# The attention rows issue in the order of the source

## The chip, the cores and the metric

The kernel runs on one core of one Trainium2 chip. The metric is the device time in microseconds of one execution. The kernel before takes 3320.47 us (median of three runs, 3319.91 to 3330.44).

## The reference, cut to what matters

Two layers follow one another on an image `x` of 256 x 256 pixels with 128 channels. Each adds its result to its input. Layer 0 is attention along each row of the image, with a bias and a gate; layer 1 is a spectral network, which the change does not touch.

```python
def _L0_conv_ref(q_x, kv_x, bias1, bias2, wq, wk, wv, wg, bg, wo, bo):
    H = 4; C_HIDDEN = 32
    q = split_heads(einsum('...qi,oi->...qo', q_x, wq)) / np.sqrt(C_HIDDEN)
    k = split_heads(einsum('...ki,oi->...ko', kv_x, wk))
    v = split_heads(einsum('...ki,oi->...ko', kv_x, wv))
    a = einsum('bshqd,bshkd->bshqk', q, k)
    a = a + bias1 + bias2
    a = softmax(a, axis=-1)
    o = einsum('bshqk,bshkd->bshqd', a, v)
    g = sigmoid(einsum('...qi,oi->...qo', q_x, wg) + bg)
    o = o * g                      # o and g laid out by head
    return einsum('...qi,oi->...qo', o, wo) + bo

x = x + _L0_conv_ref(_gn(x), kv_x, bias1, bias2, wq, wk, wv, wg, bg, wo, bo)
x = x + _L1_conv_ref(_gn(x), ...)      # layer 1, spectral
```

`s` is the row of the image: 256 independent rows, each with 256 queries, 256 keys and 4 heads.

## The kernel before, in the parts that matter

All is in 32-bit floats. Before the rows, a first stage reads the image for the group statistics (`mr`) and prepares the transposed bias as `exp(bias)` in `b1T`. Then 256 rows are worked in a software pipeline: pass `i` of the loop computes the scores of row `i`, projects row `i + 1`, transposes row `i + 2`, weighs row `i`, does the output projection of row `i - 3`, the first transform of layer 1 for row `i - 4`, and the sum over values of row `i - 1`.

```python
ps_s = tile_pool(name="l0s", bufs=1, space=PSUM)   # scores: two tiles of 128 x 1024
ps_a = tile_pool(name="l0a", bufs=4, space=PSUM)   # all else: one tag "a", four buffers

def turn(s):                                       # tr
    ps = ps_a.tile([P, 512], FP, tag="a", name=f"tr_{s}")
    for j in range(2):
        nc.tensor.transpose(ps[:, j * P : (j + 1) * P], r["x"][:, j, :], ident)
        nc.tensor.transpose(ps[:, 256 + j * P : 256 + (j + 1) * P], r["kv"][:, j, :], ident)
    nc.scalar.activation(r["xnT"], ps[:, 0:256], AF.Identity, bias=self.nmr, scale=self.mr[:, 1:2])
    nc.scalar.copy(r["kvT"], ps[:, 256:512])

def project(s):
    ps = ps_a.tile([P, 512], FP, tag="a", name=f"qk_{s}")
    nc.tensor.matmul(ps[:, 0:256], wT["wq"], xnT, start=True, stop=True)
    nc.tensor.matmul(ps[:, 256:512], wT["wk"], kvT, start=True, stop=True)
    nc.scalar.copy(r["qkT"], ps)
    ps = ps_a.tile([P, 512], FP, tag="a", name=f"gv_{s}")
    for c in range(2):
        nc.tensor.matmul(ps[:, 256 + c * P : 256 + (c + 1) * P], kvT[:, c * P : (c + 1) * P], wT["wv"], ...)
    nc.tensor.matmul(ps[:, 0:256], wT["wg"], xnT, start=True, stop=True)
    nc.vector.tensor_copy(r["v"], ps[:, 256:512])
    nc.scalar.activation(r["gate"], ps[:, 0:256], AF.Tanh, bias=self.hbg, scale=0.5)
    if s > 0:
        rows[s - 1].pop("exp")(1, 1)               # the fourth exponential of the row before

def scores(s):
    # 8 matmuls into sc[0] (heads 0, 1) and sc[1] (heads 2, 3), each by halves c of the keys
    ...
    exp(0, 0); exp(0, 1); exp(1, 0)                # on ACT; exp(1, 1) comes in project(s + 1)
    nc.vector.tensor_tensor(r["e"][0], sc[0], b1T[:, 0:2], ALU.mult)

def weigh(s):
    nc.gpsimd.tensor_tensor(e1, e1, b1T[:, 2:4], ALU.mult)
    for hp in (1, 0):
        nc.gpsimd.tensor_tensor(r["es"][hp], e[:, :, 0, :], e[:, :, 1, :], ALU.add)

def attend(s):
    ps = ps_a.tile([P, 512], FP, tag="a", name=f"av_{s}")
    # 8 matmuls of v with e into ps[:, 0:256], 4 of ones with es into ps[:, 256:512]
    ...
    nc.vector.scalar_tensor_tensor(t, r["gate"], 1.0, ps[:, 0:256], ALU.add, ALU.mult)
    nc.vector.reciprocal(rd, rd)                   # rd = ps[:, 256:512]
    nc.vector.scalar_tensor_tensor(t, rd, SUM_SCALE, t, ALU.mult, ALU.mult)
    nc.gpsimd.tensor_tensor(r["x1"], r["x"], bc(self.bo, 1, 2), ALU.add)

def out(s):                                        # ps is "wo": 2 matmuls of og with wo
    nc.vector.tensor_tensor(r["x1"], ps[:, 0:256], r["x1"], ALU.add)
    nc.sync.dma_start(self.x1d[s], r["x1"])

def spectrum(s):                                   # ps is "u": 2 transposes, 2 matmuls with adft
    nc.vector.bn_stats(self.stats2[:, s, :], ps[:, 0:256])
    nc.scalar.copy(self.U[:, :, s], ps[:, 256 : 256 + 129])
```

(Shapes are shortened, and cuts are marked with dots.) The order in which an engine gets its instructions is not the order of this text: a scheduler, working ahead of time from an estimate of each instruction's length, chooses the order on every engine and inserts the waits that data and buffers need. In each pass ScalarE (ACT in the profile) has four exponentials, the copies `qkT`, `xnT`, `kvT` and U, and the gate.

Of the kernel before, what the change touches and what calls it, by code (L numbers as in the profile page):

```python
# [11 lines left out]
AF = mybir.ActivationFunctionType  # L12
ALU = mybir.AluOpType
AX = mybir.AxisListType
PSUM = bass.MemoryType.PSUM
DRAM = bass.MemoryType.DRAM

# [141 lines left out]
class Rows:  # L159
# [4 lines left out]
    SG = 2  # L164
# [55 lines left out]
    def run(self):  # L220
        tc, NS, SG = self.tc, self.NS, self.SG
        nc = tc.nc
        ctx, wT, ident, rows = self.ctx, self.wT, self.ident, self.rows
# [5 lines left out]
        def turn(s):  # L229
            r = rows[s]  # L230
# [4 lines that stand above are left out]
            r["xnT"] = wk.tile([P, 256], FP, tag="xnT", name=f"xnT_{s}")  # L235
            nc.scalar.activation(r["xnT"], ps[:, 0:256], AF.Identity, bias=self.nmr, scale=self.mr[:, 1:2])  # L236
            r["kvT"] = wk.tile([P, 256], FP, tag="kvT", name=f"kvT_{s}")
            nc.scalar.copy(r["kvT"], ps[:, 256:512])

        def project(s):  # L240
            r = rows[s]
            xnT, kvT = r["xnT"], r["kvT"]
# [3 lines that stand above are left out]
            r["qkT"] = wk.tile([P, 512], FP, tag="qkT", name=f"qkT_{s}")  # L246
# [3 lines that stand above are left out]
                nc.tensor.matmul(  # L250
                    ps[:, 256 + c * P : 256 + (c + 1) * P], kvT[:, c * P : (c + 1) * P], wT["wv"],
                    start=True, stop=True,
                )
            nc.tensor.matmul(ps[:, 0:256], wT["wg"], xnT, start=True, stop=True)
            r["v"] = wk.tile([P, 2, P], FP, tag="v", name=f"v_{s}", bufs=3)
            nc.vector.tensor_copy(r["v"].rearrange("p c d -> p (c d)"), ps[:, 256:512])
            r["gate"] = wk.tile([P, 256], FP, tag="gate", name=f"gate_{s}", bufs=3)
            nc.scalar.activation(r["gate"], ps[:, 0:256], AF.Tanh, bias=self.hbg, scale=0.5)  # L258
            if s > 0:
                rows[s - 1].pop("exp")(1, 1)  # L260

        def scores(s):

            r = rows[s]
            qkT = r["qkT"]
            sc = [ps_s.tile([P, 2, 512], FP, tag=f"s{hp}", name=f"sc_{s}_{hp}") for hp in range(2)]
            for c in range(2):
                for h in range(4):
                    p = slice(32 * h, 32 * h + 32)
                    nc.tensor.matmul(  # L270
                        sc[h // 2][:, h % 2, c * 256 : (c + 1) * 256],
                        qkT[p, 256 + c * P : 256 + (c + 1) * P], qkT[p, 0:256],
                        start=True, stop=True,
                    )
            r["e"] = [wk.tile([P, 2, 2, 256], FP, tag=f"e{hp}", name=f"e_{s}_{hp}") for hp in range(2)]

            def exp(hp, c):
                z = sc[hp][:, :, c * 256 : (c + 1) * 256]
                nc.scalar.activation(  # L279
                    r["e"][1][:, :, c, :] if hp else z, z, AF.Exp, bias=b2T[:, c, s : s + 1]  # L280
                )

            exp(0, 0)
            exp(0, 1)
            exp(1, 0)
            r["exp"] = exp
            nc.vector.tensor_tensor(  # L287
                r["e"][0].rearrange("p h c q -> p (h c q)"), sc[0].rearrange("p h x -> p (h x)"),
                b1T[:, 0:2].rearrange("p h c q -> p (h c q)"), ALU.mult,
            )  # L290

        def weigh(s):

            r = rows[s]
            e1 = r["e"][1].rearrange("p h c q -> p (h c q)")
            nc.gpsimd.tensor_tensor(e1, e1, b1T[:, 2:4].rearrange("p h c q -> p (h c q)"), ALU.mult)  # L296
            r["es"] = [wk.tile([P, 2, 256], FP, tag=f"es{hp}", name=f"es_{s}_{hp}") for hp in range(2)]
            for hp in (1, 0):
                e = r["e"][hp]
                nc.gpsimd.tensor_tensor(r["es"][hp], e[:, :, 0, :], e[:, :, 1, :], ALU.add)  # L300

        def attend(s):
            r = rows[s]
            ps = ps_a.tile([P, 512], FP, tag="a", name=f"av_{s}")
            for c in range(2):
                for h in range(4):
                    hd = slice(32 * h, 32 * h + 32)
                    nc.tensor.matmul(  # L308
                        ps[hd, 0:256], r["v"][:, c, hd], r["e"][h // 2][:, h % 2, c, :],
                        start=(c == 0), stop=(c == 1),  # L310
                    )
            for h in range(4):
                nc.tensor.matmul(  # L313
                    ps[32 * h : 32 * h + 32, 256:512], self.ones, r["es"][h // 2][:, h % 2, :],
                    start=True, stop=True,
                )
            rd = ps[:, 256:512]
            t = r["og"] = wk.tile([P, 256], FP, tag="og", name=f"og_{s}", bufs=3)
            nc.vector.scalar_tensor_tensor(t, r["gate"], 1.0, ps[:, 0:256], ALU.add, ALU.mult)  # L319
            nc.vector.reciprocal(rd, rd)  # L320
            nc.vector.scalar_tensor_tensor(t, rd, SUM_SCALE, t, ALU.mult, ALU.mult)  # L321

            r["x1"] = wk.tile([P, 2, P], FP, tag="x1", name=f"x1_{s}", bufs=4)
            nc.gpsimd.tensor_tensor(r["x1"], r["x"], bc(self.bo, 1, 2), ALU.add)  # L324

        def out(s):
            r = rows[s]
            ps = ps_a.tile([P, 512], FP, tag="a", name=f"wo_{s}")
            for j in range(2):
                nc.tensor.matmul(  # L330
                    ps[:, j * P : (j + 1) * P], r["og"][:, j * P : (j + 1) * P], wT["wo"],
                    start=True, stop=True,
                )
            nc.vector.tensor_tensor(
                r["x1"], ps[:, 0:256].rearrange("p (j c) -> p j c", j=2), r["x1"], ALU.add
            )
            nc.sync.dma_start(self.x1d[s].rearrange("(p j) c -> p j c", j=2), r["x1"])

        def spectrum(s):
            x1 = rows[s]["x1"]  # L340
            ps = ps_a.tile([P, 512], FP, tag="a", name=f"u_{s}")
            for j in range(2):
                nc.tensor.transpose(ps[:, j * P : (j + 1) * P], x1[:, j, :], ident)
            for j in range(2):
                nc.tensor.matmul(  # L345
                    ps[:, 256 : 256 + 129], x1[:, j, :], self.adft[:, j, :], start=(j == 0), stop=(j == 1)
                )
            nc.vector.bn_stats(self.stats2[:, s, :], ps[:, 0:256])
            nc.scalar.copy(self.U[:, :, s], ps[:, 256 : 256 + 129])

        turn(0)
        turn(1)
        project(0)
        for i in range(NS + 4):
            if i % SG == 0 and i // SG + 2 < NS // SG:
                self.load(i // SG + 2)
            if i < NS:
                scores(i)
            if i + 1 < NS:
                project(i + 1)  # L360
            elif i < NS:
                rows[i].pop("exp")(1, 1)
            if i + 2 < NS:
                turn(i + 2)
            if i < NS:
                weigh(i)
            if 8 <= i < 16:
                k, h = divmod(i - 8, 4)
                nc.vector.tensor_reduce(
                    self.bad[:, k, h : h + 1], b1T[:, h].rearrange("p c q -> p (c q)"), AX.X,  # L370
                    ALU.min if k else ALU.max,
                )
            if 0 <= i - 3 < NS:
                out(i - 3)
            if 0 <= i - 4 < NS:
                spectrum(i - 4)
                del rows[i - 4]
            if 0 <= i - 1 < NS:
                attend(i - 1)


def layer0_general(tc, I, ident, x1d, U, stats2, wT, mr, bg, adft):
# [1180 lines left out]
```

## Time and profile before

| stretch, us | what it does | length |
|---|---|---|
| 0 to 110 | reads the image, statistics, bias | 110 |
| 110 to 125 | start of the row pipeline | 15 |
| 125 to 1785 | rows in steady order | 1660 |
| 1785 to 1803 | end of the row pipeline, test of the bias range | 18 |
| 1803 to 3324 | layer 1 | 1521 |

The profiled execution took 3324.3 us. PE is TensorE's matmuls and PEld its weight loads, DVE is VectorE, ACT is ScalarE, POOL is GpSimd. Over the whole span PE is busy 84% of the time, DVE 61%, POOL 47% and ACT 43%, but these are means over stages with different limits, so the stretch of the rows must be read by itself. A row of the view by lines gives an operation, its tiles (out <- in), its count, its busy time and its mean length; a row of the view of waits names the instruction that waited and the one that ended the wait. In the timeline the bracket behind an instruction gives its engine's idle time before it and who ended it. A matmul's end is modelled, so matmuls that are pipelined overlap in the listing, and starts are the safer numbers.

| operation in a row, engine | count in a row | mean ns |
|---|---|---|
| exponential in PSUM, ACT L279 | 2 | 662 |
| exponential to `e`, ACT L279 | 2 | 695 |
| product with the bias, POOL L296 | 1 | 2365 |
| sum over keys' halves, POOL L300 | 2 | 1266 |
| add of `bo`, POOL L324 | 1 | 730 |
| product with the bias, DVE L287 | 1 | 1214 |
| reciprocal, DVE L320 | 1 | 1767 |

### The profile page before, as it was taken

Reading aid. Unit: us, or ns where it says so; the run is one execution under the profiler, and the core shown is the slowest. Engines: PE = TensorE matmul, PEld = TensorE weight load, DVE = VectorE, ACT = ScalarE, POOL = GpSimd, SP = SyncE. Lnnn points to the kernel's source line nnn. Section 1 sums busy time; section 2 is a strip of 40 time slices with the busy share of each in tenths; the row PEclk is TensorE's granted clock in tenths of the full one; section 3 lists DMA queues with packets and bytes.
Section 4 is the critical chain, followed back from the end, with each engine's and each line's share of the span. In section 5 each row is a group of like instructions: output and inputs, shape, how many; then the busy total and the mean of one; then the engine's idle time right before and its main releaser. Section 6 shows DMA issues by size and latency. Waiting matters only on the chain. (4 is left out here: it accounts for less than half of the span.)

```text
span 3324.3 us, 68470 instructions
## 1 busy us (share of the span) xinstructions
PE 2783.7 (84%) x28001; PEld 1900.5 (57%) x28001; DVE 2017.9 (61%) x3107; ACT 1414.6 (43%) x2808; POOL 1559.8 (47%) x1180
## 2 busy tenths in 40 slices
PE   7899999999999999999996895979976596688666
PEld 6666766666666666667664473744433244333443
DVE  7777777777777777777777215736663253354344
ACT  0566666666666666666664101010001431244122
POOL 0588888888888888888885002000000700000001
PEclk9999999999999999999998975899987797799765
DMA  9322122222222221221220000087634824888398
GB/s 361 120 63 63 58 63 62 59 63 60 61 63 59 62 63 59 63 63 58 63 63 23 1 8 13 0 292 255 225 114 139 305 68 110 275 289 282 98 361 321
DMA packets 237699, 401.48 MB, mean 121 GB/s; under 512 B 25125, under 2 KB 184312, under 8 KB 223304
## 3 DMA queue, kind: packets, MB, share of 16 engines
q1 hardware_dynamic: 221832, 329.97, 31.2%
q0 software_dynamic: 12672, 46.14, 3.5%
q10 hardware_dynamic: 2880, 20.97, 1.5%
q8 instruction: 221, 3.62, 0.5%
q14 instruction: 94, 0.77, 0.1%
HBM read 261.20 MB, written 135.79 MB: 119 GB/s over the span
## 5 line engine op out<-in xcount | busy, mean ns | idle before, releaser
L300 POOL TENSOR_TENSOR es<-e 128x512 f32<-128x512 f32 x512 | 648.1, 1266 | 263.5 <-DVE e L287 243.5
L296 POOL TENSOR_TENSOR e<-e,b1T 128x1024 f32<-128x1024 f32 x256 | 605.5, 2365 | 0.0
L279 ACT ACTIVATE sc<-sc,b2T 128x512 f32<-128x512 f32 x512 | 339.0, 662 | 555.2 <-PE sc L270 546.9
L320 DVE RECIPROCAL av<-av 128x256 f32<-128x256 f32 x256 | 452.3, 1767 | 26.0
L308 PE MATMUL av<-e,v 128*32 128x256 f32 x4096 | 274.7, 385 | 126.1 <-ACT gate L258 125.5
L279 ACT ACTIVATE e<-sc,b2T 128x512 f32<-128x512 f32 x512 | 355.7, 695 | 0.0
L319 DVE SCALAR_TENSOR_TENSOR og<-gate,av 128x256 f32<-128x256 f32 x256 | 107.8, 421 | 406.0 <-PE av L313 405.9
L1396 POOL DMA_DIRECT2D out_dram<-x x64 | 34.0, 531 | 620.1 <-DVE x L1395 314.8
L287 DVE TENSOR_TENSOR e<-sc,b1T 128x1024 f32<-128x1024 f32 x256 | 310.7, 1214 | 5.5 <-ACT sc L279 4.8
L270 PE MATMUL sc<-qkT 32*128 32x256 f32 x4096 | 293.9, 400 | 0.4 <-DVE e L287 0.4
L1232 POOL TENSOR_TENSOR ww<-ww,xw 128x1024 f32<-128x1024 f32 x24 | 56.4, 2350 | 493.9 <-DMA xw<-x1d 481.6
L270 PEld LDWEIGHTS sc<-qkT 32*128 32x128 f32 x4096 | 185.4, 184 | 111.5 <-issue 104.4
L1070 PE MATMUL yps<-xt,mpT 128*128 128x512 f32 x512 | 230.5, 603 | 13.3 <-DMA xt<-x1d 13.3
L308 PEld LDWEIGHTS av<-e,v 128*32 128x32 f32 x4096 | 106.9, 109 | 219.2 <-ACT gate L258 173.4
L324 POOL TENSOR_TENSOR x<-xt,bo 128x256 f32<-128x256 f32 x256 | 186.7, 730 | 67.0 <-DVE mr L127 67.0
L244 PE MATMUL qk<-xnT,wT_wq 128*128 128x256 f32 x512 | 179.5, 432 | 1.7 <-ACT xnT L236 1.7
L1070 PEld LDWEIGHTS yps<-xt,mpT 128*128 128x128 f32 x512 | 95.4, 191 | 125.7 <-issue 114.1
L250 PEld LDWEIGHTS gv<-wT_wv,kvT 128*128 128x128 f32 x1024 | 155.0, 192 | 13.4
L1395 DVE TENSOR_TENSOR x<-x,blocks 128x1024 f32<-128x1024 f32 x64 | 75.6, 1221 | 139.9 <-ACT blocks L1387 133.6
L313 PE MATMUL av<-es,ones 128*32 128x256 f32 x2048 | 159.0, 379 | 1.0 <-POOL es L300 1.0
L330 PE MATMUL wo<-wT_wo,og 128*128 128x128 f32 x1024 | 156.6, 275 | 1.7 <-DVE og L321 1.7
L345 PE MATMUL u<-adft,x 128*128 128x129 f32 x1024 | 156.4, 275 | 0.0
(598 smaller groups left out, 5490.7 us busy)
## 6 DMA issues: line engine op xcount, KB each, us to landing
xb<-in_x_dram SPq DMA_DIRECT2D x32, 1024.0 KB
xt<-in_x_dram SPq DMA_DIRECT2D x128, 256.0 KB
kt<-in_L_conv_kv_x_dram SPq DMA_DIRECT2D x128, 256.0 KB
x1d<-x SPq DMA_DIRECT2D x256, 128.0 KB
xt<-x1d SPq DMA_DIRECT2D x32, 1024.0 KB
out_dram<-x POOLq DMA_DIRECT2D x64, 512.0 KB, 8.3
yd<-yt ACTq DMA_DIRECT2D x20, 1024.0 KB
x<-x1d SPq DMA_DIRECT2D x40, 512.0 KB
```

What stands on the lines that cost most here:

```text
L244: nc.tensor.matmul(ps[:, 0:256], wT["wq"], xnT, start=True, stop=True)
L270: nc.tensor.matmul(sc[h // 2][:, h % 2, c * 256 : (c + 1) * 256], qkT[p, 256 + c * P : 256 + (c + 1) * P], qkT[p, 0:256], start=True, stop ...
L279: nc.scalar.activation(r["e"][1][:, :, c, :] if hp else z, z, AF.Exp, bias=b2T[:, c, s : s + 1])
L287: nc.vector.tensor_tensor(r["e"][0].rearrange("p h c q -> p (h c q)"), sc[0].rearrange("p h x -> p (h x)"), b1T[:, 0:2].rearrange("p h c q ...
L296: nc.gpsimd.tensor_tensor(e1, e1, b1T[:, 2:4].rearrange("p h c q -> p (h c q)"), ALU.mult)
L300: nc.gpsimd.tensor_tensor(r["es"][hp], e[:, :, 0, :], e[:, :, 1, :], ALU.add)
L308: nc.tensor.matmul(ps[hd, 0:256], r["v"][:, c, hd], r["e"][h // 2][:, h % 2, c, :], start=(c == 0), stop=(c == 1),)
L313: nc.tensor.matmul(ps[32 * h : 32 * h + 32, 256:512], self.ones, r["es"][h // 2][:, h % 2, :], start=True, stop=True,)
L320: nc.vector.reciprocal(rd, rd)
L324: nc.gpsimd.tensor_tensor(r["x1"], r["x"], bc(self.bo, 1, 2), ALU.add)
L330: nc.tensor.matmul(ps[:, j * P : (j + 1) * P], r["og"][:, j * P : (j + 1) * P], wT["wo"], start=True, stop=True,)
L1070: nc.tensor.matmul(ps[j].rearrange("p (n w) -> p n w", w=W), mpT[:, sc, tt], by_turn(xt[:, sc])[:, j], start=(sc == 0), stop=False,)
```

## The change

The row loop is wrapped in a block of manual scheduling for four engines: TensorE, ScalarE, VectorE and GpSimd. Inside it these engines get their instructions in the order in which the source makes them. The scheduler keeps inserting the waits, and the queue of the transfers (SyncE) is still ordered by it. On ScalarE the source has the gate directly behind the copy `qkT`, ahead of the fourth exponential. The aim is to have the gate done early, as it reads a PSUM tile whose buffer is used again. Nothing of the computation changes.

```diff
+ENG = mybir.EngineType
...
-        turn(0)
-        turn(1)
-        project(0)
-        for i in range(NS + 4):
-            if i % SG == 0 and i // SG + 2 < NS // SG:
-                self.load(i // SG + 2)
-            if i < NS:
-                scores(i)
-            if i + 1 < NS:
-                project(i + 1)
... (the rest of the loop, likewise)
+        with tc.manual_schedule(engines={ENG.PE, ENG.Activation, ENG.DVE, ENG.Pool}):
+            turn(0)
+            turn(1)
+            project(0)
+            for i in range(NS + 4):
+                if i % SG == 0 and i // SG + 2 < NS // SG:
+                    self.load(i // SG + 2)
+                if i < NS:
+                    scores(i)
+                if i + 1 < NS:
+                    project(i + 1)
+                elif i < NS:
+                    rows[i].pop("exp")(1, 1)
+                if i + 2 < NS:
+                    turn(i + 2)
+                if i < NS:
+                    weigh(i)
+                if 8 <= i < 16:
+                    k, h = divmod(i - 8, 4)
+                    nc.vector.tensor_reduce(
+                        self.bad[:, k, h : h + 1], b1T[:, h].rearrange("p c q -> p (c q)"), AX.X,
+                        ALU.min if k else ALU.max,
+                    )
+                if 0 <= i - 3 < NS:
+                    out(i - 3)
+                if 0 <= i - 4 < NS:
+                    spectrum(i - 4)
+                    del rows[i - 4]
+                if 0 <= i - 1 < NS:
+                    attend(i - 1)
```

More of the change, by code (lines that the diff above doesn't have):

```diff
@@ L349, in spectrum @@
             nc.scalar.copy(self.U[:, :, s], ps[:, 256 : 256 + 129])
-        turn(0)
-        turn(1)
-        project(0)
-        for i in range(NS + 4):
-            if i % SG == 0 and i // SG + 2 < NS // SG:
-                self.load(i // SG + 2)
-            if i < NS:
-                scores(i)
-            if i + 1 < NS:
-                project(i + 1)
[L361 to L379, printed above, removed]
+        with tc.manual_schedule(engines={ENG.PE, ENG.Activation, ENG.DVE, ENG.Pool}):
[28 more added lines that the diff above has]
+                    attend(i - 1)
 def layer0_general(tc, I, ident, x1d, U, stats2, wT, mr, bg, adft):
```

## The prediction, made before the changed kernel ran

> **What bounds the kernel now.** I read the table of slices first (TensorE at nine tenths or more from slice 3 to slice 21, with its clock granted in full), then the busy time of stretches, to separate the attention rows from what stands before and behind them:
>
> ```profile
> 125.00:1785.00 1660.00, 1534.37 (x16194) 1152.87 (x16189) 1221.52 (x1770) 1105.23 (x2275) 1402.52 (x1011) 1.00 0.20 61
> ```
>
> (Length of the stretch; busy time and number of instructions of TensorE's matmuls, its weight loads, VectorE, ScalarE and GpSimd; clock, DMA share, GB/s.) The rows take half of the kernel. In them TensorE is busy 92% of the time, GpSimd 84%, VectorE 74%, ScalarE 67%, and the DMA engines a fifth. So transfers do not bound them, and TensorE nearly does, but not quite. The view of waits for the same stretch says who it waits for:
>
> ```profile
> ACT sc L279 <- PE sc L270: 545.1, 253, 2.4
> DVE og L319 <- PE av L313: 403.8, 254, 1.6
> ...
> PE av L308 <- ACT gate L258: 125.5, 250, 0.5
> ```
>
> (Total us, times, longest us.) ScalarE and VectorE have idle time left, up to 2.4 and 1.6 us in a row, and GpSimd (a line left out) up to 1.2. TensorE has one wait, 0.50 us in each of 250 rows: the product of weights and values (`av`) waits for the gate's tanh. Yet `av` does not read the gate. The reason is a buffer: all small PSUM tiles share one tag with four buffers, six are taken per row in the order qk, gv, tr, wo, u, av, and so `av` takes the buffer that `gv` gave up, four tiles before. The gate is `gv`'s last reader. One row in order of time, first ScalarE's instructions, then TensorE's (columns: start, length, engine, line, operation):
>
> ```profile
> 1004.24 1.36 ACT L279 ACTIVATE sc<-sc,b2T 128x512 f32<-128x512 f32 x2 [2.16 <-PE sc L270]
> 1005.52 0.68 ACT L279 ACTIVATE e<-sc,b2T 128x512 f32<-128x512 f32 x1
> 1006.09 0.59 ACT L247 COPY qkT<-qk 128x512 f32<-128x512 f32 x1
> 1006.56 0.71 ACT L279 ACTIVATE e<-sc,b2T 128x512 f32<-128x512 f32 x1
> 1007.14 0.59 ACT L236 ACTIVATE xnT<-tr,nmr,mr 128x256 f32<-128x256 f32 x1
> 1007.59 0.50 ACT L258 ACTIVATE gate<-gv,hbg 128x256 f32<-128x256 f32 x1
> ...
> 1010.81 1.36 ACT L279 ACTIVATE sc<-sc,b2T 128x512 f32<-128x512 f32 x2 [2.17 <-PE sc L270]
> ```
>
> ```profile
> 1005.49 0.60 PE L254 MATMUL gv<-xnT,wT_wg 128*128 128x256 f32 x2
> ...
> 1007.03 0.61 PE L345 MATMUL u<-adft,x 128*128 128x129 f32 x4
> 1008.14 1.07 PE L308 MATMUL av<-e,v 128*32 128x256 f32 x16 [0.50 <-ACT gate L258]
> 1009.03 0.61 PE L313 MATMUL av<-es,ones 128*32 128x256 f32 x8
> 1009.57 1.15 PE L270 MATMUL sc<-qkT 32*128 32x256 f32 x16
> ```
>
> The row repeats every 6.57 us (1010.81 less 1004.24). The gate's input is ready at 1006.09 (L254's end), but it starts at 1007.59, behind the last exponential and the copy of `xnT` on ScalarE. That is a closed **loop**: `av` to the next scores 1.43 (1008.14 to 1009.57), scores to the first exponential 1.24 (1009.57 to 1010.81), three exponentials 1.85 (1004.24 to 1006.09), start of `qkT` to start of the last exponential 0.47, that to `xnT` 0.58, `xnT` to gate 0.45, the gate 0.50, and 0.05 to `av`: 6.57. The loop accounts for the whole period.
>
> **What the Trainium skill says.** PSUM — Partial Sum Buffer, "Engine vs sequencer instructions": the queues of ScalarE, VectorE and GpSimd are strictly first in, first out. The trace agrees: the ready gate sits 1.50 us behind two others. Perfetto Trace Analysis, "Optimization Strategy": the same gap repeating on the engine that should be full can mean too little PSUM for the next tile. It agrees, 250 gaps of 0.50 us. ScalarE: Activation LUTs, "Table sets: the hidden batching unit": exp and tanh lie in one table set. It agrees: the gate's line has one table load (1.28 us) for 256 gates, so moving a tanh among exponentials costs no load. GPSIMD Engine Reference, "8. Key points": GpSimd shares its SBUF interfaces with VectorE, and suffers from VectorE instructions with two SBUF inputs. VectorE's row instructions each read at least one operand in PSUM or only one tensor, and GpSimd's sums take 1266 ns whatever stands beside them. I therefore leave GpSimd's lengths as they are in the new order.
>
> **The change part by part.** It adds and removes no instruction of the computation; it fixes the order on four engines.
>
> TensorE: the trace already has the source's order in a row (scores, qk, gv, tr, wo, u, av). Nothing moves: 0.
>
> ScalarE: the source has exponentials 1 to 3, `qkT`, gate, exponential 4, `xnT`, `kvT`, U. Only the gate moves, ahead of exponential 4 and `xnT`. The loop above loses 0.58 + 0.45 = 1.03 and becomes 1.43 + 1.24 + 1.85 + 0.47 + 0.50 + 0.05 = **5.54 us**. The next loops then count:
>
> - TensorE's own work. The trace has rows that did not wait. At the start, before any `u` exists:
>
> ```profile
> 130.31 1.15 PE L270 MATMUL sc<-qkT 32*128 32x256 f32 x16
> ...
> 133.67 0.61 PE L330 MATMUL wo<-wT_wo,og 128*128 128x128 f32 x4
> 134.21 1.07 PE L308 MATMUL av<-e,v 128*32 128x256 f32 x16
> ...
> 135.65 1.15 PE L270 MATMUL sc<-qkT 32*128 32x256 f32 x16
> ```
>
> 5.34 us from scores to scores, with 0.54 from `wo` to `av`. With `u` in between, the full row (`wo` at 1006.36, `u` at 1006.81, L345 at 1007.03) has `wo` to `u` 0.45, 0.22 to L345, and from L345 to `av` again 0.54 (four matmuls of nearly the same width): 1.21 in place of 0.54, so 5.34 + 0.67 = **6.01 us**.
> - Scores, three exponentials, `qkT`, `u` (which takes qk's buffer), `av`, scores: 1.24 + 1.85 + 0.59 + 0.05 to `u`, then 0.22 + 0.54 to `av`, 1.43 to scores: 5.92.
> - VectorE: `og` at 1003.14 to the end of `v` at 1007.35 is 4.21 (product, reciprocal, product, bias product, copy), 0.05 to `av`, which is also behind this last reader of `gv`, and 1.57 from `av` to `og` (1008.14 to 1009.71): 5.83.
> - GpSimd: from `es` at 1007.10 to the end of `x` at 1012.72 is 5.62 of work.
>
> The largest is TensorE's 6.01. Of the 1.03 us that the gate gains, TensorE can use 6.57 - 6.01 = **0.56 us** a row. That is more than the 0.50 of the wait, because the modelled end of the matmuls hides a piece of it.
>
> GpSimd: the source takes the product first, then both sums, where the scheduler put the sum that needs only VectorE's half first. The product starts with the end of exponential 4, about 0.45 later than before. Counted from the scores: the gate starts at 3.56 (1.24 + 1.85 + 0.47), exponential 4 at 4.0, its end at 4.7, product to 7.1, sums to 9.6. `av` of that row comes one period later, at 6.0 + 4.5 = 10.5, and its sums at 11.4. So 1.8 us are left: 0.
>
> VectorE: the cyclic order is the same. But the eight reductions that watch the bias, which the scheduler had put at 39 to 54 us, now stand in rows 8 to 15: 8 x 0.68 = 5.4 us. They stand behind `v`, so they delay no buffer of `gv`, and VectorE has some 1.0 us of its 1.6 left there. I count 0.
>
> Sum: 250 rows x 0.56 = 140 us. 3320.5 - 140 = **3180 us**, and layer 1 as it was.
>
> **The rivals.** (1) GpSimd becomes the bound: 5.62 of 6.01 is 94% full, and its product now starts later. If sums were late by 0.3 us, the row would be 6.3, the kernel 3255. Against it: the slack of 1.8 us and lengths that did not vary. (2) Another wait takes the gate's place: the copy `v` or `qkT` ends within 0.1 to 0.2 us of the need, and three loops lie within 0.2 us of each other. If their meeting costs 0.15 us a row, the period is 6.15 and the kernel 3215. This I think the likeliest miss. (3) The fixed order costs at the edges: the start and the drain of the pipeline, where the scheduler had filled gaps (GpSimd's first four bias sums, the eight reductions). The stretches before 125 and behind 1785 us give at most 5 to 10 us. (4) The fixed order goes wrong in the engines' waits, ScalarE being held by a gate that waits for TensorE. The gate's input is ready 0.47 us before its new turn, so it would need a slower TensorE; that would give 3320 or more.
>
> **Range and chances.** If TensorE's own work came out at the next loop's 5.92, the kernel would be 3320 - 250 x 0.65 = 3158. Rival 2 gives 3215. Range 3152 to 3218. Faster by over 2% means under 3254, a period under 6.31: 0.90. Within 2%: rival 1, 0.06. Slower: 0.04, for something in the order of buffers that the source doesn't show.
>
> **What would show it.** Period near 6.0; `av` no longer waiting for the gate; gate directly after `qkT` in the timeline; TensorE above 98% in the rows; GpSimd's wait for VectorE's `e` gone, and in its place one for ScalarE's last exponential; VectorE's wait for `av` about 1.0 us. I am wrong if TensorE has a new wait (for `v`, `qkT`, or GpSimd's `es`), if its clock drops below 1.00 in the rows, or if layer 1 moved.

## The result, and the profile after

The changed kernel takes 3272.22 us against 3322.27 before: a ratio of 0.984 (95% interval 0.982 to 0.987). 3180 us was predicted, with a range from 3152 to 3218. So 50 us came of the 140 that were counted on. The profiled execution fell from 3324.3 to 3265.5 us, and 55 us of these 59 lie in the rows: the small product that ends them (`fps`) starts at 1748.6 us in place of 1803.4. Layer 1 did not change beyond what repeated runs differ by.

The busy time of the rows after the change, in the columns of the prediction:

```profile
125.00:1730.00 1605.00, 1535.74 (x16202) 1153.89 (x16198) 1226.84 (x1779) 1128.53 (x2277) 1405.34 (x1014) 1.00 0.20 63
```

TensorE does the same 1535 us of work in 1605 in place of 1660 us. It is busy 96% of the time and not all of it. The waits of the same stretch:

```profile
DVE og L320 <- PE av L314: 342.6, 253, 1.5
ACT sc L280 <- PE sc L271: 290.3, 254, 1.4
POOL e L297 <- ACT e L280: 179.8, 251, 1.0
ACT gate L259 <- DVE v L257: 179.0, 253, 1.0
...
PE av L309 <- ACT gate L259: 69.1, 250, 0.5
```

The fourth line is new: the gate waits for VectorE's copy `v`, 0.71 us a row. And the last line is still there: `av` still waits for the gate in 250 rows, now 0.28 us each in place of 0.50. One row on ScalarE, on VectorE and on TensorE:

```profile
1005.59 1.36 ACT L280 ACTIVATE sc<-sc,b2T 128x512 f32<-128x512 f32 x2 [1.14 <-PE sc L271]
...
1007.43 0.58 ACT L248 COPY qkT<-qk 128x512 f32<-128x512 f32 x1
1008.73 0.47 ACT L259 ACTIVATE gate<-gv,hbg 128x256 f32<-128x256 f32 x1 [0.71 <-DVE v L257]
1009.10 0.68 ACT L280 ACTIVATE e<-sc,b2T 128x512 f32<-128x512 f32 x1
```

```profile
1004.48 0.42 DVE L320 SCALAR_TENSOR_TENSOR og<-gate,av 128x256 f32<-128x256 f32 x1 [1.38 <-PE av L314]
1005.00 1.77 DVE L321 RECIPROCAL av<-av 128x256 f32<-128x256 f32 x1
1006.81 0.42 DVE L322 SCALAR_TENSOR_TENSOR og<-av,og 128x256 f32<-128x256 f32 x1
1007.15 1.21 DVE L288 TENSOR_TENSOR e<-sc,b1T 128x1024 f32<-128x1024 f32 x1
1008.28 0.41 DVE L257 COPY v<-gv 128x256 f32<-128x256 f32 x1
...
1010.82 0.42 DVE L320 SCALAR_TENSOR_TENSOR og<-gate,av 128x256 f32<-128x256 f32 x1 [1.38 <-PE av L314]
```

```profile
1006.83 0.60 PE L255 MATMUL gv<-xnT,wT_wg 128*128 128x256 f32 x2
...
1009.25 1.07 PE L309 MATMUL av<-e,v 128*32 128x256 f32 x16 [0.28 <-ACT gate L259]
```

The gate is next in ScalarE's queue when `qkT` is done (1008.01), and its projection is ready at 1007.43, but it starts at 1008.73, just behind the end of `v` at 1008.69. The two read different halves of the one PSUM tile `gv`. The new loop runs through both: `og` to the end of `v` 4.21 (1004.48 to 1008.69), 0.04 to the gate, the gate 0.47, 0.05 to `av`, and `av` to `og` 1.57 (1009.25 to 1010.82). That is 6.34 us, and the rows repeat every 6.34 us (1004.48 to 1010.82).

The Trainium skill has the rule that I had not applied: PSUM — Partial Sum Buffer, "PSUM bank collisions raise a hardware error", says that two engines must not access one bank in the same partitions at one time, that two readers collide as well, ScalarE with VectorE, and that the compiler's scheduler adds a dependency between them. The wait of 0.71 us between the readers of two halves of one tile agrees with such a dependency. That the bank is its reason is not shown: no run here lets the two read together, and none gives the halves tiles of their own.

### The profile page after: what moved, and what is told of

It reads as the page before. It is cut to its first block, busy times and chain, and to the rows that moved or that the text cites. A ratio compares the mean times of both kernels' runs of the same rounds, so it can differ in the third digit from the quotient of the medians.

```text
span 3265.5 us, 68862 instructions
## 1 busy us (share of the span) xinstructions
PE 2776.0 (85%) x28001; PEld 1901.6 (58%) x28001; DVE 2018.8 (62%) x3107; ACT 1436.8 (44%) x2808; POOL 1561.5 (48%) x1180
## 5 line engine op out<-in xcount | busy, mean ns | idle before, releaser
L301 POOL TENSOR_TENSOR es<-e 128x512 f32<-128x512 f32 x512 | 641.3, 1273 | 20.1
L280 ACT ACTIVATE e<-sc,b2T 128x512 f32<-128x512 f32 x512 | 347.8, 680 | 0.0
L259 ACT ACTIVATE gate<-gv,hbg 128x256 f32<-128x256 f32 x256 | 121.1, 473 | 180.5 <-DVE v L257 180.5
```

The costliest lines, as they stand in the source:

```text
L280: nc.scalar.activation(r["e"][1][:, :, c, :] if hp else z, z, AF.Exp, bias=b2T[:, c, s : s + 1])
```

## The experiments

**1. The gate ahead of the copy of `v` in the source.**

```diff
             nc.tensor.matmul(ps[:, 0:256], wT["wg"], xnT, start=True, stop=True)
+            r["gate"] = wk.tile([P, 256], FP, tag="gate", name=f"gate_{s}", bufs=3)
+            nc.scalar.activation(r["gate"], ps[:, 0:256], AF.Tanh, bias=self.hbg, scale=0.5)
             r["v"] = wk.tile([P, 2, P], FP, tag="v", name=f"v_{s}", bufs=3)
             nc.vector.tensor_copy(r["v"].rearrange("p c d -> p (c d)"), ps[:, 256:512])
-            r["gate"] = wk.tile([P, 256], FP, tag="gate", name=f"gate_{s}", bufs=3)
-            nc.scalar.activation(r["gate"], ps[:, 0:256], AF.Tanh, bias=self.hbg, scale=0.5)
```

> The changed kernel with the gate's tanh ahead of the copy of v in the source: both read the same PSUM bank, so now v waits for the gate and not the gate for v. Theory (the gate stands behind v only because the two share a bank; the loop og to v 4.21, gate 0.5, av to og 1.57 makes 6.34 us a row): VectorE's loop falls back to 5.83, the longest is TensorE's 6.01, and the kernel takes about 3190 us (3272 - 250 x 0.33). Rival (VectorE's chain up to v is itself the bound, the gate is beside it): v ends later than before, so 3272 us or more. Rival (the order on GpSimd is the bound): no change, 3272 us.

Measured: 3182.35 us, 0.956 of the kernel before (0.954 to 0.958). The rows' busy time, then ScalarE's and VectorE's lines in one row:

```profile
125.00:1640.00 1515.00, 1514.90 (x16174) 1151.53 (x16173) 1227.28 (x1777) 1105.17 (x2273) 1405.35 (x1013) 1.00 0.21 66
```

```profile
1005.96 0.59 ACT L248 COPY qkT<-qk 128x512 f32<-128x512 f32 x1
1006.43 0.50 ACT L258 ACTIVATE gate<-gv,hbg 128x256 f32<-128x256 f32 x1
1006.80 0.71 ACT L280 ACTIVATE e<-sc,b2T 128x512 f32<-128x512 f32 x1
```

```profile
1005.61 1.21 DVE L288 TENSOR_TENSOR e<-sc,b1T 128x1024 f32<-128x1024 f32 x1
1006.96 0.42 DVE L259 COPY v<-gv 128x256 f32<-128x256 f32 x1
```

The gate now follows `qkT` at once and ends at 1006.93. The copy `v` starts at 1006.96, some 0.2 us later than VectorE could have (`v` followed `e` by 1.13 us in the changed kernel, by 1.35 here). TensorE is busy in all of the 1515 us (matmuls that overlap in the listing count once), and the list of waits has none of its matmuls for another engine left. The rows repeat every 6.00 us (`qkT` at 1005.96 and 1011.96). Both rivals fall: counted from the start of `qkT`, `v` ends at 1.42 us here and at 1.26 in the changed kernel, and yet this kernel is faster; and GpSimd's order is unchanged.

**2. Manual order on ScalarE alone.**

```diff
-        with tc.manual_schedule(engines={ENG.PE, ENG.Activation, ENG.DVE, ENG.Pool}):
+        with tc.manual_schedule(engines={ENG.Activation}):
```

> Manual order for ScalarE alone; TensorE, VectorE and GpSimd ordered by the scheduler. Theory (the place of the gate on ScalarE is all that counts): as the changed kernel, 3272 us within 8. Rival (the fixed order on GpSimd or VectorE brings a part of the gain, or costs a part of what was expected): different by 15 us or more, to either side.

Measured: 3266.62 us, 0.982 (0.980 to 0.984), with rows of 6.34 us (`qkT` at 1004.09 and 1010.43). It is the changed kernel's time within the intervals of the two. GpSimd here has the scheduler's order and waits for VectorE's `e` again (0.65 us a row), and the time differs by less than 6 us.

**3. The gate taken of SBUF.** The tanh is taken of `xnT`, so the gate's projection is made and not used, and the output is another.

```diff
-            nc.scalar.activation(r["gate"], ps[:, 0:256], AF.Tanh, bias=self.hbg, scale=0.5)
+            nc.scalar.activation(r["gate"], xnT, AF.Tanh, bias=self.hbg, scale=0.5)
```

> The changed kernel with the gate's tanh taken of xnT in SBUF in place of the gate's projection in PSUM: the projection is still made but not used, so the output differs. The gate then has no tie to the PSUM bank. Theory (the shared bank costs the 0.33 us a row that the prediction missed): av waits for v alone, TensorE's 6.01 us is the bound, about 3190 us. Rival (VectorE's chain up to v is the bound): 3272 us. If this comes out at about 3190 and the kernel with the gate ahead of v does too, TensorE's 6.01 is the floor.

Measured: 3183.15 us, 0.956 (0.955 to 0.958). With `v` in its old place and no tie between the gate and the bank, the row is 6.00 us as in the first experiment. The wait for `v` is gone from ScalarE; the waits of the rows (125 to 1640 us) begin:

```profile
ACT sc L280 <- PE sc L271: 392.9, 253, 1.9
DVE og L320 <- PE av L314: 256.4, 253, 1.1
```

and no line of the kind "gate behind v" or "av behind gate" follows. TensorE is busy in 1514.8 of the 1515 us from 125 to 1640. Turning the tie round and taking it away end at the same time, so TensorE's 6.00 us is the floor of this row.

**4. The gate back behind `xnT`, with all four engines still in the order of the source.**

```diff
             r["gate"] = wk.tile([P, 256], FP, tag="gate", name=f"gate_{s}", bufs=3)
-            nc.scalar.activation(r["gate"], ps[:, 0:256], AF.Tanh, bias=self.hbg, scale=0.5)
+            hbg, gate = self.hbg, r["gate"]
+            r["late"] = lambda: nc.scalar.activation(gate, ps[:, 0:256], AF.Tanh, bias=hbg, scale=0.5)
...
             nc.scalar.activation(r["xnT"], ps[:, 0:256], AF.Identity, bias=self.nmr, scale=self.mr[:, 1:2])
+            if "late" in rows.get(s - 1, {}):
+                rows[s - 1].pop("late")()
             r["kvT"] = wk.tile([P, 256], FP, tag="kvT", name=f"kvT_{s}")
```

(Row 0 and the last row, which have no such neighbour, call it at once.)

> The changed kernel with the gate put back behind the copy of xnT on ScalarE (fourth exponential, xnT, gate, kvT), all four engines still in the order of the source. Theory (only the place of the gate counts): as the kernel before, 3322 us within 8, with the row at 6.57. Rival (the order on GpSimd, or the reductions in rows 8 to 15, count): different by 15 us or more.

Measured: 3325.98 us, 1.000 (0.999 to 1.001), with rows of 6.57 us. Together with the second experiment: the place of the gate on ScalarE is the whole effect of the change, and the new order on GpSimd, the eight reductions in rows 8 to 15 and the edges of the rows cost or bring nothing beyond some 6 us.

**5. The sum over values earlier in each pass.**

```diff
+                if 0 <= i - 1 < NS:
+                    attend(i - 1)
                 if 0 <= i - 3 < NS:
                     out(i - 3)
                 if 0 <= i - 4 < NS:
                     spectrum(i - 4)
                     del rows[i - 4]
-                if 0 <= i - 1 < NS:
-                    attend(i - 1)
```

> The changed kernel with the sum over values moved ahead of the output projection and the first transform in each pass, so that av is the fourth small tile behind the u of the row before and takes its buffer, long free; now u takes the buffer of gv, some 1.9 us later in TensorE's order. Gate and copy of v stay in their places, the gate still waits for v. Theory (the 0.33 us a row is a wait for a buffer and nothing that av reads): no wait for the gate is left, TensorE's own 6.0 to 6.1 us is the bound (one change of the array's tiling more in a row), 3190 to 3215 us. Rival (VectorE's chain through v and the gate must end before av in any case): 3272 us or more.

Measured: 3367.05 us, 1.013 (1.012 to 1.015): slower than both. The expectation missed. The wait of `av` for the gate is gone, as the theory of the buffer has it, but another stands in its place. The first lines of the waits (from 125 to 1740 us), and ScalarE at the turn of a row:

```profile
ACT U L350 <- DVE stats L349: 410.0, 237, 2.4
DVE e L288 <- POOL es L301: 399.5, 236, 2.1
```

```profile
1008.38 0.39 ACT L350 COPY U<-u 128x129 f32<-128x129 f32 x1 [1.93 <-DVE stats L349]
1008.56 1.39 ACT L280 ACTIVATE sc<-sc,b2T 128x512 f32<-128x512 f32 x2
```

It is the same tie in another tile: the statistics of `u` on VectorE and the copy U on ScalarE read one tile, the statistics come first in the source, and in this order they are VectorE's last work of a row. ScalarE's queue then holds the next row's exponentials behind U. The second line could not be taken at its word: VectorE starts `e` at 1010.04, 0.09 us after the two exponentials end (1008.56 + 1.39 = 1009.95), while GpSimd's two sums run from 1008.24 to 1010.75. The time alone would also fit the rival, which said 3272 us or more. The eighth experiment tells these apart.

**6. The gate ahead of `v`, without manual scheduling.** The kernel before, with the edit of the first experiment alone.

> The kernel before, without manual scheduling, with the gate written ahead of the copy of v. The scheduler then puts the fourth exponential, the gate and xnT in this order on ScalarE, and v waits for the gate. Theory (loop of durations: scores 1.24, exponentials 1.85, qkT to the fourth 0.47, that to the gate 0.58, gate 0.50, 0.05, v 0.41, 0.05, av to scores 1.43 = 6.58 us): as the kernel before, 3325 us within 10. Rival (exchanging the two readers is by itself what brings the gain, wherever the gate stands on ScalarE): about 3185 us.

Measured: 3325.92 us, 1.000 (0.999 to 1.001). The rows repeat every 6.58 us (`qkT` at 1006.71 and 1013.29), the figure that the loop in the expectation gives. The tie now acts the other way about, and TensorE waits for `v` as long as it had waited for the gate:

```profile
DVE v L258 <- ACT gate L257: 180.6, 254, 0.8
PEld av L308 <- DVE v L258: 175.0, 250, 0.7
PE av L308 <- DVE v L258: 127.2, 250, 0.5
```

So neither half is worth anything like the whole: the gate's early place alone brings 50 us, the exchange alone nothing, and both together 140. The same loop tells how closely that fits: with the gate ahead of the fourth exponential, as in experiment 1, the 0.58 from that exponential to the gate falls out, and 6.58 becomes 6.00, which is TensorE's own row. In experiment 1 the tie is thus still there; it ends just in time, without slack that these figures show.

**7. The gate ahead of `v`, with manual order on ScalarE alone.** The first experiment with the edit of the second.

> Gate ahead of the copy of v, with manual order on ScalarE alone; the other three engines are left to the scheduler, which fills the start and the end of the rows better. Theory (TensorE's 6.0 us is the bound in the rows, as with manual order on four engines): 3177 us within 6, some 5 less than with four engines. Rival (GpSimd's order counts once the row is at 6.0 us, as it is then 93% full): different from the four-engine kernel's 3182 by 15 us or more.

Measured: 3182.64 us, 0.958 (0.956 to 0.959), the time of the four-engine kernel, so GpSimd's order doesn't count at 6.00 us a row either. The 5 us that I expected of better edges are not there.

**8. The early sum over values, with U ahead of the statistics.** The edit of the fifth experiment, and in `spectrum`:

```diff
+            nc.scalar.copy(self.U[:, :, s], ps[:, 256 : 256 + 129])
             nc.vector.bn_stats(self.stats2[:, s, :], ps[:, 0:256])
-            nc.scalar.copy(self.U[:, :, s], ps[:, 256 : 256 + 129])
```

> The kernel with the early sum over values (3367 us), with the copy U written ahead of the statistics of u, which share its PSUM bank. In that kernel U stood behind the statistics, these at the end of VectorE's row, and ScalarE held the next row's exponentials behind U (a loop of 6.5 to 6.9 us). Theory (the order of two readers of one bank, the same as with v and the gate, made that kernel slow): U waits for TensorE alone, the row falls to 6.05 to 6.2 us, where TensorE's own work and GpSimd's last sum are close together: 3200 to 3240 us, and av waits for no gate. Rival (GpSimd's sums, which VectorE is recorded to wait for, hold the row): 3340 us or more. Rival (the chain through v and the gate bounds wherever av stands): about 3272 us or more.

Measured: 3231.24 us, 0.973 (0.971 to 0.974), with a row of 6.19 us. Exchanging two readers of one tile takes 136 us off the fifth experiment's time, and VectorE's `e` waits for GpSimd's sums 4.3 us in all in place of 399.5. The gate still waits for `v` 0.60 us a row, and it holds `av` no longer:

```profile
DVE og L320 <- PE av L314: 193.7, 253, 1.9
ACT sc L280 <- PE sc L271: 189.7, 252, 1.8
ACT gate L259 <- DVE v L257: 152.5, 253, 1.0
```

```profile
1005.46 1.07 PE L309 MATMUL av<-e,v 128*32 128x256 f32 x16
1006.29 0.47 ACT L259 ACTIVATE gate<-gv,hbg 128x256 f32<-128x256 f32 x1 [0.60 <-DVE v L257]
```

Here `av` runs before the gate of the same pass has started. This shows that `av`'s wait was for a buffer and for nothing that it reads. The row is 6.19 us and not 6.00 for TensorE's own work: it is busy in 1564.3 of the 1565 us from 125 to 1690. Its starts differ from those of experiment 1 at two places only: the last transpose to the next matmul takes 0.20 us in place of 0.11, where `av` follows and not `wo`, and `wo` to `u` takes 0.55 in place of 0.45, where `wo` stands behind `av`. At both TensorE now changes between whole-array and tiled matmuls; that this change is the reason is likely, and not shown.

## Why the prediction was wrong, by its own steps

- **What bounds the kernel: right.** The loop through the gate explained 6.57 us, and putting the gate back (experiment 4) gives 6.57 again.
- **The gate's gain on ScalarE: wrong, and this is the step that failed.** "The loop above loses 0.58 + 0.45 = 1.03 and becomes" 5.54 us took the gate to be free as soon as `qkT` was done. It is free when `v` is done: it started at 1008.73, 0.72 us after `qkT`. The signs to look for missed the place as well: they named a new wait on TensorE, and the new wait stood on ScalarE. I had the place of `v` in front of me: VectorE's loop was worked out as 5.83 with `v` as "this last reader of `gv`", side by side with the gate, when the two stand one behind the other. With 0.04 and the gate's 0.47 in series between `v` and `av`, the same loop is 5.83 + 0.51 = 6.34 us. The gain is 6.57 - 6.34 = 0.23 us in each of 250 rows, 57 us, against 50 to 59 measured. The missing term was 0.33 us a row, 82 us, and it is what experiments 1 and 3 gave back (90 and 89 us).
- **The trace before could have told.** In steady rows the gate stood so late that `v` was always done, so the tie left no wait. In the row that the prediction shows, the gate starts at 1007.59, and VectorE's copy ends at 1007.35:

```profile
1006.94 0.41 DVE L256 COPY v<-gv 128x256 f32<-128x256 f32 x1
```

In the first row, where the gate was not late, the tie did leave a wait. VectorE and ScalarE at the start of the kernel before:

```profile
115.80 0.42 DVE L256 COPY v<-gv 128x256 f32<-128x256 f32 x1 [4.60 <-PE gv L254]
114.69 1.28 ACT L258 ACT_TABLE_LOAD   x1
116.26 0.47 ACT L258 ACTIVATE gate<-gv,hbg 128x256 f32<-128x256 f32 x1 [0.28 <-DVE v L256]
```

TensorE's last matmul of `gv` (L254, the gate's own input) releases the copy at 115.80, and the table load ends at 115.97. The gate still waits 0.28 us, for a copy that it does not read.
- **TensorE's own 6.01 us: right.** Once the gate no longer holds `av` behind `v`, the row is 6.00 us, and the kernel 3182 us (experiment 1) or 3183 (experiment 3), where 3180 was computed for that row. Loops that lie close to TensorE's meet it without a cost of their own: the predicted 5.83 and 5.92 in experiment 3, and in experiment 1 the one of 6.00 through the gate and `v`.
- **GpSimd and VectorE at no cost: right.** GpSimd waits for the last exponential and not for `e`, as expected, and experiments 2 and 4 show that neither its order nor the reductions count.
- **The rivals.** The second, "another wait takes the gate's place", is the one that came, but I gave it 0.15 us a row for a chance meeting of loops. It was a fixed dependency of 0.33.
- **The chances.** I put 0.06 on a change within 2%, and put it down to GpSimd. The measured ratio lies there, at 0.984, for another reason.

## What to carry to other kernels

When an instruction is moved forward in a queue, list all that it waits for in the program and not only what the trace shows it waiting for: a dependency that is always met by the time the instruction's turn comes leaves no mark until the move. In these kernels two engines that empty two halves of one PSUM tile worked one behind the other in the order of the source, so put first the reader whose engine is free first, and work out the loop with both in series. Here that exchange, worth nothing alone, made the change worth 140 us in place of 50.

## What was not expected of the hardware

- The dependency between two readers of one tile costs hardly more than the first reader's own time, whichever comes first: 0.04 us from the end of `v` to the gate (changed kernel), 0.03 us from the end of the gate to `v` (experiment 1).
- In experiment 3 three loops, 5.83, 5.92 and 6.01 us by the prediction's sums, lie within 0.2 us of one another, and the rows ran at the longest. TensorE was busy in 1514.8 of 1515 us, so nothing was lost to their nearness.
- The tanh over 256 columns took 473 ns when ScalarE had stood idle before it (changed kernel), about 500 ns directly behind another instruction (before), and 528 ns when it read SBUF (experiment 3). The starts of neighbours are therefore the safer measure of what an instruction costs in a queue: from the gate's start to the next exponential's it is 0.37 us in the changed kernel and in experiment 1 alike.
